# The last phase of a four-stage recurrent kernel: batches taken in pairs, gate products in seven block products, copies on ScalarE

## The chip, the cores and the metric

The kernel runs on one core of one Trainium2 chip. The metric is the device time of one execution in microseconds; the time before is the median of three runs, 1617.33 us (1615.9 to 1617.58).

## The reference, cut to what matters

Everything is float32, with batch 16, sequence 512 and width 512. Four residual stages follow one another.

```python
x = x + L0(x, cond)      # becomes x * (gate + 2): one multiplication in the kernel
x = x + L1(x, cond)      # h_t = tanh(x_t @ Wx + b + h_{t-1} @ Wh), 512 steps
x = x + L2(x, cond)      # gated linear recurrence, below
x = x + L3(x, cond)      # a layer of its own for every batch, below

# L2
f = sigmoid(x @ W_f.T + b_f); i = sigmoid(x @ W_i.T + b_i)
s = f + i + 1e-8
f, i = f / s, i / s
new = i * (x @ W_h.T + b_h)
log_cum = cumsum(log(f + 1e-8))
hidden = cumsum(exp(log_cum[-1] - padded(log_cum)[:-1]) * new) + exp(log_cum) * cond

# L3: rank-8 factors x_a, x_b of every batch from a small network over cond
layer = base + x_a @ x_b.T          # 512 x 512, per batch
out = x + x @ layer
```

Below, x2 is the sequence after L1 and x3 the one after L2.

## The kernel before

The kernel has two long parts. Widths lie on the 128 partitions in four chunks (`KC` = 4), time and batch on the free axis.

**The recurrence** (the loop over `n` in 64 blocks and `s` in 8 steps, up to about 909 us). At each step TensorE multiplies the state with `wh_sb` (L417), ScalarE takes the tanh (L609), VectorE transposes the result in four pieces (L610) and, at four of the eight steps, adds the states of two time steps into the tile x2 (L622), which stays in SBUF whole (16 batches of 4 x 512). TensorE's spare time in a step goes to the input products of a later block and to `early_gate`: the first steps of the gates of L2, for which x2 is already known. `SETS` says which, and `made_before(b, j)` returns the number of steps that batch b and chunk j have behind them (128 to 192). These normalized gates go to DRAM (`early`) through SP's queue. The order of instructions on TensorE, ScalarE, VectorE and SP is the order in which the code records them (`manual_schedule`); each of these engines works through its own list in order, and so does Pool.

**The last phase** takes one batch after the other, and in it four gate units (`gate_unit`, one for each chunk j of the output width). A unit makes three products (forget, input, candidate) of four matmuls each over the steps that are not made yet, into PSUM banks. ScalarE takes two sigmoids out of PSUM (L716) into `f` and `i`; SP fetches the early steps of both from DRAM (L715). VectorE then runs the chain L717 to L732: sum, reciprocal, normalization, candidate (read from PSUM, L722), three scans with a multiplication between them (L726, L729, L730, L732). Pool adds the two parts and x2 (L736, L737), which makes x3.

After the second unit of a batch, the output tiles of the batch before follow on TensorE: four tiles of four matmuls (L756), each copied out by ScalarE (L751) and stored by SP (L752) through two buffers `osb`. After the third unit the layer of this batch is made (`layer_of`: four rank-8 products, L535, and VectorE's addition of the base out of PSUM, L539). The first layer is made in the last step of the recurrence. The last batch's output is split so that only the last quarter of its products waits for the last chain.

Of the kernel before, what the change touches and what calls it, by code (L numbers as in the profile page):

```python
# [74 lines left out]
IDLE = (3, 12, 2)  # L75
EPS = 1e-8
# [7 lines left out]
def kernel(  # L84
# [47 lines left out]
    bias_a = dram.tile([R, D], F32, name="bias_a")  # L132
    factor = [dram.tile([BP, R, D], F32, name=f"factor_{i}") for i in range(2)]
# [311 lines left out]
    def early_gate(q, step):  # L445
# [18 lines left out]
        for c in range(KC):  # L464
            nc.tensor.matmul(  # L465
                ps[c * BP : (c + 1) * BP, :].rearrange("p (b t) -> p b t", **shape),
                w[:, k, j * P + c * BP : j * P + (c + 1) * BP],
                x2[:, k, batches, steps],
                start=(k == 0),
                stop=(k == KC - 1),  # L470
                skip_group_check=True,
            )
# [64 lines left out]
    def add_base(banks, layer):  # L537
        for c, pl in enumerate(banks):
            nc.vector.tensor_tensor(layer[:, c, :], pl, base_sb[:, c, :], ALU.add)  # L539

# [13 lines left out]
    BEGINS = {T - 1: 0, 0: 1, 2: 2}  # L556

# [7 lines left out]
    for n in range(NBLK):  # L565
# [3 lines left out]
        for s in range(T):  # L569
# [21 lines left out]
            if (n, s) == (NBLK - 1, T - 1):  # L591


                first_layer = [
                    new_bank(NBLK, i, "pl").rearrange("p g f -> p (g f)") for i in range(NBANK)
                ]
                first_layer.append(ps_q.tile([P, D], F32, tag="pg", name="pl_3"))
                make_layer(*first_rows, first_layer)
# [15 lines left out]
            if n == 0 and s == G - 1:  # L614
                opening.close()
                x2pool = ctx.enter_context(tc.tile_pool(name="x2pool", bufs=1, side="right"))
                x2 = x2pool.tile([P, KC, B, S], F32)
            if s == max(PAIRS[g]):
                t0, t1 = PAIRS[g]
                step = t1 - t0  # L620
                at = slice(n * T + t0, n * T + t1 + step // abs(step), step)
                nc.vector.tensor_tensor(  # L622
                    x2[:, :, :, at].rearrange("p k b t -> p k t b"),
                    xs[n][:, :, t0 // 2, :, :],
                    turned.rearrange("p k (t b) -> p k t b", t=2),
                    ALU.add,
                )
            elif n + 2 < NBLK:
                gated(nc.vector, xs[n + 2], xb, s)
# [25 lines left out]
            if (n, s) == (1, 0):  # L655

                end_layer(0)

# [10 lines left out]
        if n == NBLK - 4:  # L669
            at = w2pool.tile([P, P], F32, tag="b2", name="at_0", bufs=2)  # L670
            bt = w2pool.tile([P, D], F32, tag="w2", name="bt_0", bufs=AHEAD)
            first_rows = load_layer(0, at, bt)
        pre, nxt = nxt, ahead
    while urgent or pieces:
        do_pieces(S)

    add_base(first_layer, wx_sb)
    rnn.close()

    x3pool = ctx.enter_context(tc.tile_pool(name="x3pool", bufs=2))  # L680
    work = ctx.enter_context(tc.tile_pool(name="work", bufs=2))
    zero = work.tile([P, 1], F32, bufs=1)
    nc.gpsimd.memset(zero, 0.0)  # L683
    zeros = zero.to_broadcast([P, S])

    pools = {
        tag: ctx.enter_context(tc.tile_pool(name=f"ps_{tag}", bufs=1, space=PSUM))
        for tag in ("pl0", "pf", "pl1", "pi", "po0", "pc0", "po1", "pc1")
# [5 lines left out]
    def gate_unit(b, j, x3):  # L694
        ps = []
        te = made_before(b, j)
        for w_sb, tag in ((wf_sb, "pf"), (wi_sb, "pi"), (wc_sb, f"pc{j % 2}")):
            p = bank(tag, f"{b}_{j}")
            for k in range(KC):
                nc.tensor.matmul(  # L700
                    p[:, te:],
                    w_sb[:, k, j * P : (j + 1) * P],
                    x2[:, k, b, te:],
                    start=(k == 0),
                    stop=(k == KC - 1),
                )
            ps.append(p)
        pf, pi, pc = ps

        f = work.tile([P, S], F32, tag="f", name=f"f_{b}_{j}", bufs=3)  # L710
        i = work.tile([P, S], F32, tag="i", name=f"i_{b}_{j}")
        s = work.tile([P, S], F32, tag="s", name=f"s_{b}_{j}")
        old, new = slice(0, te), slice(te, S)
        for which, (gate, p, bias) in enumerate(((f, pf, C_BF), (i, pi, C_BI))):
            nc.sync.dma_start(out=gate[:, old], in_=early[b, which, j, :, old])  # L715
            nc.scalar.activation(gate[:, new], p[:, new], AF.Sigmoid, bias=col(bias, j))  # L716
        nc.vector.scalar_tensor_tensor(s[:, new], f[:, new], EPS, i[:, new], ALU.add, ALU.add)  # L717
        nc.vector.reciprocal(s[:, new], s[:, new])  # L718
        nc.vector.tensor_tensor(f[:, new], f[:, new], s[:, new], ALU.mult)
        nc.vector.tensor_scalar(f, f, EPS, None, ALU.add)  # L720
        nc.vector.tensor_tensor(i[:, new], i[:, new], s[:, new], ALU.mult)
        nc.vector.scalar_tensor_tensor(  # L722
            i[:, new], pc[:, new], col(C_BH, j), i[:, new], ALU.add, ALU.mult
        )

        nc.vector.tensor_tensor_scan(  # L726
            s[:, ::-1], f[:, ::-1], zeros, 1.0, ALU.mult, ALU.add
        )
        nc.vector.tensor_tensor(i, i, s, ALU.mult)  # L729
        nc.vector.tensor_tensor_scan(s, i, zeros, 0.0, ALU.add, ALU.add)  # L730

        nc.vector.tensor_tensor_scan(  # L732
            f, f, zeros, condT_sb[:, j, b : b + 1], ALU.mult, ALU.add
        )
        engine = nc.vector if (b, j) == (B - 1, KC - 1) else nc.gpsimd
        engine.tensor_tensor(s, s, f, ALU.add)  # L736
        engine.tensor_tensor(x3[:, j, :], s, x2[:, j, b, :], ALU.add)  # L737

    def layer_rows(b):
        at = work.tile([P, P], F32, tag="at", name=f"at_{b}", bufs=1)  # L740
        bt = work.tile([P, D], F32, tag="bt", name=f"bt_{b}", bufs=1)
        return load_layer(b, at, bt)

    def layer_of(b, at, bt, layer):
        banks = [bank(tag, f"{b}_layer") for tag in ("pl0", "pl1", "po0", "po1")]
        make_layer(at, bt, banks)
        add_base(banks, layer)

    def leave(b, t, po, tag="osb"):
        osb = work.tile([P, D], F32, tag=tag, name=f"osb_{b}_{t}")  # L750
# [3 lines left out]
    def output_part(po, t, x3, layer, ks):  # L754
        for k in ks:
            nc.tensor.matmul(  # L756
                po, x3[:, k, t * P : (t + 1) * P], layer[:, k, :], start=(k == 0), stop=(k == KC - 1)
            )

    def last_layer(b, x3, layer):  # L760
        for t in range(S // P):
            po = bank(f"po{t % 2}", f"{b}_{t}")
            output_part(po, t, x3, layer, range(KC))
            leave(b, t, po)

    layer = wx_sb
    pending = None
    for b in range(B):
        x3 = x3pool.tile([P, KC, S], F32, tag="x3", name=f"x3_{b}")
        end = b == B - 1  # L770
        if 0 < b < B - 1:
            factors = layer_rows(b)
        for j in range(KC):
            gate_unit(b, j, x3)
            if j == (KC - 1 if end else 1) and pending is not None:
                last_layer(*pending)
            if j == 2 and 0 < b < B - 1:
                layer_of(b, *factors, layer)
            if j == 0 and end:

                layer_of(B - 1, *layer_rows(B - 1), base_sb)
        pending = b, x3, layer


    last = S // P - 1
    pos = [bank(tag, "last") for tag in ("pl0", "pl1", "po0")]
    ends = [bank(tag, "end")[:, : D // 2] for tag in ("po1", "pi")]
    columns = [slice(n * D // 2, (n + 1) * D // 2) for n in range(2)]

    def last_rows(ks, n):  # L790
        for k in ks:
            nc.tensor.matmul(
                ends[n],
                x3[:, k, last * P :],
                base_sb[:, k, columns[n]],
                start=(k == 0),
                stop=(k == KC - 1),
            )

    for t, po in enumerate(pos):  # L800
        output_part(po, t, x3, base_sb, range(KC - 1))
    for n in range(2):
        last_rows(range(KC - 1), n)

    for t, po in enumerate(pos):
        output_part(po, t, x3, base_sb, (KC - 1,))
        leave(B - 1, t, po, ("osb", "i", "s")[t])
    for n, copy in enumerate((nc.vector.tensor_copy, nc.scalar.copy)):
        last_rows((KC - 1,), n)
        osb = work.tile([P, D // 2], F32, tag=("s", "osb")[n], name=f"osb_end_{n}")  # L810
        copy(osb, ends[n])
        (nc.sync, nc.scalar)[n].dma_start(out=out[B - 1, last * P :, columns[n]], in_=osb)


# [56 lines left out]
```

## Time and profile before

| | |
|---|---|
| median of three runs | 1617.33 us |
| span of the profiled execution | 1614.1 us (the 3.2 us beside it are start and end) |
| end of the recurrence (last addition into x2) | 909.25 us |
| last phase, from there to the end of the span | 704.8 us |
| busy share of TensorE, VectorE, ScalarE, Pool over the span | 99%, 70%, 26%, 11% |
| one batch of the last phase, start to start of the output tiles | 45.0 us (batches 1 to 7), 42.4 us (later) |
| granted clock of TensorE | 1.00 throughout |

A line of a group or a timeline names the start and the length in us, the engine, the line of the code, the operation, the tiles it writes and reads with their sizes, the number of records taken together, and in brackets how long the engine stood idle before and what it waited for. PE is TensorE, PEld its weight loads, DVE VectorE, ACT ScalarE, POOL GpSimd, SPq the queue of SP that issues transfers.

### The profile page before, as it was taken

The numbers are of one execution on the slowest core, as the hardware profiler recorded it, in microseconds if no ns is written. First come the engines' busy times: TensorE is split into PE (matmuls) and PEld (weight loads), VectorE is DVE, ScalarE is ACT, GpSimd is POOL, SyncE is SP. The second block draws the span as 40 slices with busy tenths as digits, with TensorE's granted clock in tenths as the row PEclk, the third lists the DMA queues.
The fourth block names the chain that finished last, engine by engine and source line by source line (L and its number), as shares of the span: only waits on it lengthen the run. The fifth ranks groups of instructions, "written<-read, shape, count | busy, mean of one in ns | idle before, by whom it ended". The sixth has DMA issues, their size and how long they took to land.

```text
span 1614.1 us, 67901 instructions
## 1 busy us (share of the span) xinstructions
PE 1603.6 (99%) x29328; PEld 1146.0 (71%) x29328; DVE 1132.3 (70%) x3618; ACT 424.9 (26%) x2484; POOL 172.6 (11%) x145
## 2 busy tenths in 40 slices
PE   9999999999999999999999999999999999999998
PEld 6888888888888888888888655555555555555564
DVE  4555655565556666666665798888888888988887
ACT  3333333333333333333333211111111111111111
POOL 0000000000000000000000022222222222222222
PEclk9999999999999999999999999999999999999999
DMA  7554431111111111111111101111111111111111
GB/s 228 148 147 128 121 105 46 36 31 36 37 37 37 37 37 37 37 37 31 37 39 30 29 21 43 33 43 39 43 40 44 44 46 39 31 44 47 37 44 58
DMA packets 128085, 88.11 MB, mean 55 GB/s; under 512 B 22645, under 2 KB 116633, under 8 KB 127785
## 3 DMA queue, kind: packets, MB, share of 16 engines
q1 hardware_dynamic: 79152, 55.05, 11.1%
q10 hardware_dynamic: 48632, 28.73, 6.2%
q8 instruction: 229, 3.75, 1.0%
q14 instruction: 72, 0.58, 0.1%
HBM read 55.67 MB, written 28.07 MB: 52 GB/s over the span
## 4 chain that ended last, share of the span: by engine, by line
PE 96%; DVE 2%; DMA 1%; issue 0%; SPq 0%; ACT 0%; ACTq 0%; DVEq 0%
PE pre L417 41%; PE po L756 13%; PE pg L465 13%; PE pf L700 9%; PE pc L700 9%; PE pi L700 9%; PE pf L380 1%; PE pl_layer L535 1%; DVE s L718 1%; DMA wh_sb<-in_wh_dram 1%; PE pl_last L756 0%; DMA xb<-in_xT_dram 0%; DVE s L726 0%; DVE s L730 0%; PE po_last L756 0%
## 5 line engine op out<-in xcount | busy, mean ns | idle before, releaser
L417 PEld LDWEIGHTS pre<-wh_sb,h_out 128*32 128x32 f32 x16384 | 466.7, 110 | 146.6 <-DVE h_out L610 143.4
L417 PE MATMUL pre<-wh_sb,h_out 128*32 128x128 f32 x16384 | 560.6, 273 | 2.4 <-DVE h_out L610 1.1
L610 DVE STREAM_TRANSPOSE h_out<-a 128x32 f32<-128x32 f32 x2048 | 264.6, 187 | 347.4 <-ACT a L609 345.9
L609 ACT ACTIVATE a<-pre 128x32 f32<-128x32 f32 x2048 | 238.0, 203 | 573.4 <-PE pre L417 572.7
L417 PE MATMUL pre<-wx_sb,x 128*32 128x128 f32 x8192 | 285.9, 273 | 1.0 <-DMA wx_sb<-in_wx_dram 0.5
L417 PEld LDWEIGHTS pre<-wx_sb,x 128*32 128x32 f32 x8192 | 239.0, 110 | 2.1 <-DMA wx_sb<-in_wx_dram 1.5
L756 PE MATMUL po<-wx_sb,x 128*128 128x512 f32 x480 | 209.0, 592 | 0.1
L756 PEld LDWEIGHTS po<-wx_sb,x 128*128 128x128 f32 x480 | 91.0, 190 | 111.6 <-issue 105.7
L700 PE MATMUL pf<-x,wf_sb 128*128 128x352 f32 (+3 forms) x512 | 165.3, 466 | 0.3 <-DVE x L622 0.3
L700 PE MATMUL pc<-x,wc_sb 128*128 128x352 f32 (+3 forms) x512 | 163.7, 463 | 1.3 <-DVE i L722 1.3
L700 PE MATMUL pi<-x,wi_sb 128*128 128x352 f32 (+3 forms) x512 | 163.6, 462 | 0.0
L718 DVE RECIPROCAL s<-s 128x368 f32<-128x368 f32 (+2 forms) x64 | 152.2, 2378 | 2.2
L700 PEld LDWEIGHTS pf<-x,wf_sb 128*128 128x128 f32 x512 | 96.0, 190 | 68.4 <-issue 15.8
L736 POOL TENSOR_TENSOR s<-s,f 128x512 f32<-128x512 f32 x63 | 86.5, 1374 | 509.9 <-DVE s L730 504.1
L700 PEld LDWEIGHTS pc<-x,wc_sb 128*128 128x128 f32 x512 | 97.2, 190 | 57.5 <-DVE i L722 1.9
L700 PEld LDWEIGHTS pi<-x,wi_sb 128*128 128x128 f32 x512 | 97.3, 190 | 55.9
L622 DVE TENSOR_TENSOR x<-x,h_out 128x128 f32<-128x128 f32 x256 | 101.2, 395 | 18.9 <-DMA wi_sb<-in_wiT_dram 0.2
L751 ACT COPY osb<-po 128x512 f32<-128x512 f32 x60 | 35.1, 585 | 263.4 <-PE po L756 144.9
L683 POOL MEMSET zero<- 128x1 f32 x1 | 0.1, 98 | 907.5 <-DVE wx_sb L539 907.5
L717 DVE SCALAR_TENSOR_TENSOR s<-f,i 128x368 f32<-128x368 f32 (+2 forms) x64 | 34.7, 543 | 88.1 <-ACT i L716 88.1
L716 ACT ACTIVATE f<-pf,vec_sb 128x368 f32<-128x368 f32 (+2 forms) x64 | 35.7, 558 | 215.2 <-PE pf L700 160.6
L465 PE MATMUL pg<-x,wc_sb 128*32 128x512 f32 (+1 forms) x640 | 84.2, 581 | 0.0
(113 smaller groups left out, 1270.8 us busy)
## 6 DMA issues: line engine op xcount, KB each, us to landing
out_dram<-osb SPq DMA_DIRECT2D x63, 256.0 KB
xb<-in_xT_dram ACTq DMA_DIRECT2D x61, 256.0 KB
w<-in_l3w_dram SPq DMA_DIRECT2D x72, 128.0 KB
w<-in_l3w_dram ACTq DMA_DIRECT2D x64, 128.0 KB
early<-ef SPq DMA_DIRECT2D x39, 128.0 KB
early<-ei SPq DMA_DIRECT2D x39, 128.0 KB
f<-early SPq DMA_DIRECT2D x16, 96.0 KB
i<-early SPq DMA_DIRECT2D x16, 96.0 KB
```

The source lines that it names most:

```text
L417: nc.tensor.matmul(pre[PLACE[g][0]][j * BP : (j + 1) * BP, PLACE[g][1], :], lhsT, tile_columns(w, j), start=False, stop=False, skip_group_ ...
L465: nc.tensor.matmul(ps[c * BP : (c + 1) * BP, :].rearrange("p (b t) -> p b t", **shape), w[:, k, j * P + c * BP : j * P + (c + 1) * BP], x2 ...
L609: nc.scalar.activation(a[:, at], pre[bank][:, place, at], AF.Tanh)
L610: nc.vector.transpose(turned[:, c, :], a[:, at])
L622: nc.vector.tensor_tensor(x2[:, :, :, at].rearrange("p k b t -> p k t b"), xs[n][:, :, t0 // 2, :, :], turned.rearrange("p k (t b) -> p k ...
L700: nc.tensor.matmul(p[:, te:], w_sb[:, k, j * P : (j + 1) * P], x2[:, k, b, te:], start=(k == 0), stop=(k == KC - 1),)
L716: nc.scalar.activation(gate[:, new], p[:, new], AF.Sigmoid, bias=col(bias, j))
L717: nc.vector.scalar_tensor_tensor(s[:, new], f[:, new], EPS, i[:, new], ALU.add, ALU.add)
L718: nc.vector.reciprocal(s[:, new], s[:, new])
L736: engine.tensor_tensor(s, s, f, ALU.add)
L751: nc.scalar.copy(osb, po)
L756: nc.tensor.matmul(po, x3[:, k, t * P : (t + 1) * P], layer[:, k, :], start=(k == 0), stop=(k == KC - 1))
```

## The change

Only the last phase is written anew; the recurrence gets another layout of x2 and stores.

- **Pairs and seven products.** Two batches are one left operand of two rows, the two halves of the width its two columns; the weights are a 2 x 2 block matrix. Six units a pair: F0 to F3 join the forget and input weights of a chunk, C0 and C2 the candidate weights of two chunks. A unit makes seven block products of two matmuls instead of eight. The four sums of input blocks are made once a pair (`sums_of`, on Pool, between the products of F3 of the pair before; on VectorE for pair 0), the combined weights once, in place (`make_weights`).
- **Running sums in PSUM, copied out.** Products 1, 6, 7, 4 add up in one bank (`al`), 5 and 3 in another (`be`), 2 stands alone (`ga`). After each product ScalarE copies the running sum to SBUF: into `got` (1, 6, 7) or `rest` (5, 2, 3). `add` then adds `rest` to `got`: on VectorE for F units, on Pool for C units. `rest_ring` has one buffer, the other rings have two. Two sets of banks (`al0`, `be0`, `ga0` and `al1`, `be1`, `ga1`) alternate between units.
- **The chain** works on two batches at once up to the scans, then six scans; the second scan multiplies inside, and the multiplication that stood between the scans goes to Pool with the two additions, three Pool instructions for two batches.
- **Layers** are copied from PSUM by ScalarE and the base is added by Pool; the fourth bank of a layer is `po1`. Output tiles are spread over the units as fillers, one quarter at each 0 of `USUAL`. The first layer moves from the recurrence into the last phase.
- **x2 in DRAM.** x2 is now laid out batch first. Batches 6 to 15 are also stored to `kept` during and after the recurrence (`keep_part`, on SP's queue); their place in SBUF becomes working memory, and five pairs are fetched back into a ring of four slots. x3 of a pair overwrites x2 of the pair before.

The diff, cut to its core:

```diff
+    def keep_part(batches, steps):
+        nc.sync.dma_start(out=kept[...], in_=x2[:, batches, :, steps])
+    keeping = {}
+    for first, part in enumerate((slice(0, 128), slice(128, 256), slice(256, 384))):
+        for b in range(KEPT, B):
+            keeping[20 + 14 * first + b - KEPT, 6] = slice(b, b + 1), part
+    for b in range(KEPT, B):
+        keeping[60 + (b - KEPT) // 4, 2 * ((b - KEPT) % 4)] = slice(b, b + 1), slice(384, 480)
...
-                x2 = x2pool.tile([P, KC, B, S], F32)
+                x2 = x2pool.tile([P, B, KC, S], F32)
...
+            if (n, s) in keeping:
+                keep_part(*keeping[n, s])
...
+    for b in (*range(KEPT + 2, B, 2), KEPT):
+        keep_part(slice(b, b + 2), slice(480, S))
...
+    f_ring = Ring(carve(2, S), carve(2, S))
+    four_ring = Ring(four_a, carve(4, NB))
+    three_ring = Ring(three_a, carve(3, NB))
+    rest_ring = Ring(rest_a)
+    osb_ring = Ring(carve(D), carve(D))
...
+        def product(self, which):
+            ...
+            ps = {1: self.al, 6: self.al, 7: self.al, 4: self.al, 5: self.be, 3: self.be, 2: self.ga}[which]
+            for k in range(2):
+                nc.tensor.matmul(ps, w[:, k, :], src[:, k, :], start=(k == 0 and which in (1, 5, 2)), ...)
+            if which == 4:
+                if self.gates:
+                    nc.scalar.activation(self.f[:, 1, new], ps, AF.Sigmoid, bias=col(C_BF, self.j))
+                else:
+                    nc.scalar.copy(self.got[:, 2, n], ps)
+                return
+            to = {1: self.spots[0], 6: self.spots[1], 7: self.spots[2],
+                  2: self.rest[:, 0], 3: self.rest[:, 1], 5: self.rest[:, 2]}[which]
+            nc.scalar.copy(to[:, n], ps)
+        def add(self):
+            if self.gates:
+                nc.vector.tensor_tensor(self.got[:, :, n], self.got[:, :, n], self.rest[:, :, n], ALU.add)
+            else:
+                nc.gpsimd.tensor_tensor(two, two, self.rest[:, 0:2, n], ALU.add)
+                nc.gpsimd.tensor_tensor(one, one, self.rest[:, 2, n], ALU.add)
+        def squash(self):
+            nc.scalar.activation(self.f[:, 0, new], self.got[:, 0, n], AF.Sigmoid, bias=col(C_BF, j))
+            nc.scalar.activation(self.i[:, :, new], self.got[:, 1:3, n], AF.Sigmoid, bias=col(C_BI, j))
...
+    def chain(unit, cand_unit, final=False):
+        v = nc.vector
+        v.scalar_tensor_tensor(s[:, :, new], f[:, :, new], EPS, i[:, :, new], ALU.add, ALU.add)
+        v.reciprocal(s[:, :, new], s[:, :, new])
+        v.tensor_tensor(f[:, :, new], f[:, :, new], s[:, :, new], ALU.mult)
+        v.tensor_scalar(f, f, EPS, None, ALU.add)
+        v.tensor_tensor(i[:, :, new], i[:, :, new], s[:, :, new], ALU.mult)
+        v.scalar_tensor_tensor(i[:, :, new], cand, col(C_BH, j), i[:, :, new], ALU.add, ALU.mult)
+        for b in range(2):
+            v.tensor_tensor_scan(s[:, b, ::-1], f[:, b, ::-1], zeros, 1.0, ALU.mult, ALU.add)
+            v.tensor_tensor_scan(i[:, b], i[:, b], f[:, b], 0.0, ALU.add, ALU.mult)
+            v.tensor_tensor_scan(f[:, b], f[:, b], zeros, condT_sb[...], ALU.mult, ALU.add)
+            if not final and b == 0:
+                continue
+            ...
+            e.tensor_tensor(i[:, at, : S - 1], i[:, at, : S - 1], s[:, at, 1:], ALU.mult)
+            e.tensor_tensor(i[:, at], i[:, at], f[:, at], ALU.add)
+            e.tensor_tensor(x3[:, at, j, :], i[:, at], x[:, at, j, :], ALU.add)
...
+    USUAL = (1, 5, 0, 6, 2, 0, 7, 3, 0, 4, 0)
...
+            c0 = new("C0")
+            queue_tile(6, p - 2)
+            run(c0, USUAL, {2: [before["F3"].squash]})
+            fill(4)
+            chain(before["F3"], before["C2"])
+            c0.add()
+            f0 = new("F0")
+            queue_tile(7, p - 2)
+            run(f0, USUAL)
+            fill(4)
+            f0.add()
+        f1 = new("F1")
+        queue_tile(0, p - 1)
+        run(f1, USUAL, {2: [f0.squash]} if p else {})
+        fill(4)
+        chain(f0, c0)
+        f1.add()
+        if p:
+            layer_of(2 * p - 1, sides[0])
+            queue_tile(1, p - 1)
+            fill(4)
+        c2 = new("C2")
+        queue_tile(2, p - 1)
+        run(c2, USUAL, {2: [f1.squash]})
+        fill(4)
+        chain(f1, c0)
+        c2.add()
+        f2 = new("F2")
+        queue_tile(3, p - 1)
+        run(f2, USUAL)
+        fill(4)
+        f2.add()
+        f3 = new("F3")
+        queue_tile(4, p - 1)
+        hooks = {2: [f2.squash]}
+        ...                                  # sums of the next pair, on Pool
+        run(f3, USUAL, hooks)
+        fill(4)
+        chain(f2, c2)
+        f3.add()
+        layer_of(2 * p, sides[0])
+        queue_tile(5, p - 1)
+        fill(4)
```

`run` records a unit's products in the order of `USUAL`; a 0 stands for one quarter of an output tile, and a hook is recorded right after the copy of the product whose number it has.

## The prediction

> **What bounds the kernel now.** I read the page's busy times first, then the chain that ended last, then the timeline of the last phase (from 909.4 us on) engine by engine. Busy time, then the chain's two lines:
>
> ```profile
> PE 1603.6 (99%) x29328; PEld 1146.0 (71%) x29328; DVE 1132.3 (70%) x3618; ACT 424.9 (26%) x2484; POOL 172.6 (11%) x145
> ...
> PE 96%; DVE 2%; DMA 1%; issue 0%; SPq 0%; ACT 0%; ACTq 0%; DVEq 0%
> ```
>
> TensorE never rests, in the recurrence or after it. The last phase in one stretch (length, then busy PE, PEld, DVE, ACT, POOL, then clock, DMA share, GB/s):
>
> ```profile
> 930.00:1290.00 360.00, 360.00 (x1098) 197.99 (x1097) 306.77 (x354) 54.50 (x97) 88.64 (x66) 1.00 0.12 39
> ```
>
> PE 100%, VectorE 85%, Pool 25%, ScalarE 15%: an edit that takes products away helps only while VectorE, and what is handed between engines, keeps pace. TensorE's timeline for part of a batch:
>
> ```profile
> 1127.22 2.74 PE L700 MATMUL pf<-x,wf_sb 128*128 128x384 f32 x8
> 1129.80 2.74 PE L700 MATMUL pi<-x,wi_sb 128*128 128x384 f32 x8
> ...
> 1134.96 13.90 PE L756 MATMUL po<-wx_sb,x 128*128 128x512 f32 x32
> 1148.69 2.64 PE L700 MATMUL pf<-x,wf_sb 128*128 128x368 f32 x8
> ```
>
> A matmul of the code is two records. From start to start, four of 384 columns take 2.58 us (0.645 each, 1.68 ns a column) and sixteen of 512 take 13.73 (0.858 each). VectorE's timeline of one gate unit (one batch, one chunk, 384 columns):
>
> ```profile
> 915.45 0.56 DVE L717 SCALAR_TENSOR_TENSOR s<-f,i 128x384 f32<-128x384 f32 x1 [2.88 <-ACT i L716]
> 916.04 2.55 DVE L718 RECIPROCAL s<-s 128x384 f32<-128x384 f32 x1
> ...
> 921.69 0.69 DVE L729 TENSOR_TENSOR i<-i,s 128x512 f32<-128x512 f32 x1
> 922.29 1.28 DVE L732 TENSOR_TENSOR_SCAN f<-f,condT_sb,zero 128x512 f32<-128x512 f32 x1
> ...
> 924.61 0.53 DVE L717 SCALAR_TENSOR_TENSOR s<-f,i 128x384 f32<-128x384 f32 x1
> ```
>
> One unit is 9.16 us, L717 to L717.
>
> **Products: -56 us of TensorE.** Before, columns of gate products sum to 273,408 (12 a unit, widths 512 minus `made_before`). After: six units a pair, seven products of two matmuls, 240,128. At 1.68 ns: 458 against 402 us. Output tiles (256 matmuls, 219.7 us) and layers (about 1.07 us each) stay. TensorE's own sum is 402 + 220 + 17 = 639 us, against the 704.7 that the phase takes now.
>
> **VectorE: less in all, but in bigger lumps.** A chain now serves two batches. Two units of 9.16 are 18.3; two L729 leave for Pool (0.6 each, start to start), and six instructions start once instead of twice (about 0.1 each): 16.4 us at 384 columns, 15.0 at 320. Each F unit adds one addition of 1152 columns, 1.3 us (1.04 ns a column, from 0.55 us at 384). Layer additions (0.65 us each) go to Pool. Some 69 us a pair: alone no bound.
>
> **The wait that the change adds.** `rest_ring` holds one buffer. Every unit's copy of product 5 writes it, so it waits until the unit before has been added. For C units that addition stands on Pool, in order behind the three Pool instructions of a chain, and these wait for that chain's last scans on VectorE. The built program shows it: the copy of product 5 of F0 and of F2 waits for Pool, and on ScalarE the copies of products 6 and 7 are queued behind it; TensorE's product 7 accumulates onto the bank that copy 6 must first empty, and everything of TensorE's is behind product 7. So two times a pair the engines run one after another. At 384 columns, from one squash to the next but one:
>
> - squash on ScalarE, 0.58 and 0.90 us, overlapping: 1.3
> - chain on VectorE: 16.4
> - Pool: three of 1024 columns and C's addition of 1152. The two rows (minimum/median/maximum):
>
> ```profile
> L736 POOL TENSOR_TENSOR s<-s,f x60: 1260/1425/1501, 933.9 to 1574.8; 128x512 f32<-128x512 f32 x60
> L737 POOL TENSOR_TENSOR x<-s,x x63: 1260/1266/1432, 926.3 to 1595.1; 128x512 f32<-128x512 f32 x63
> ```
>
>   At 1.26 us for 512: 3 x 2.52 + 2.8 = 10.4. At L736's median it would be 11.7.
> - two copies on ScalarE: 0.9
> - TensorE: products 7, 3, 4, then 1, 5, 6, 2 of the next unit (7 x 1.29) and three quarters of a tile (3 x 0.86), then a copy of 0.5: 12.1
> - hand-overs, six of about 0.08: 0.5. Sum 41.6.
> - then the next squash 1.3, chain 16.4, F1's addition 1.3 (on VectorE, behind the chain) and the copies of products 5, 6 and 2 behind it, 1.3: 20.3. TensorE has one unit, a layer and a tile beside this, 18: hidden.
>
> 61.9 us for half a pair, which is one batch; a batch takes 45.0 now (output groups start 45.0 apart early, 42.4 later). The second half with 368 and 352 columns gives 59 to 60, so a pair 121; the later pairs (320 columns first) 115.
>
> The Trainium skill ("GPSIMD Engine Reference", Specifications) says that Pool shares its SBUF interfaces with VectorE and suffers from instructions with two inputs there. L736's 1.43 beside L737's 1.27 agrees. In the stretch that counts VectorE stands idle, so I take the lower row; the upper adds 16 x 1.3 = 21 us.
>
> **Start, first pairs, end.** Pair 0 has no tiles and only one such hand-over (C2 to F2), but VectorE first builds the combined weights (24 subtractions of 256 columns at 0.34; the 16 last ones delay the first chain by 5.5). First chain at 18, two chains with addition and squash 35, Pool and copies 12, then the rest of F2, F3 and the layer 13: about 80. Pair 1: 121 plus 5, since its first tile needs pair 0's last chain. After pair 7: two tiles, a layer and 32 output matmuls (36 us) around the last chain, then 4 for copy and store (now 1610.5 to the end): 49 with some waiting. Sum: 80 + 126 + 2 x 121 + 4 x 115 + 49 = 957 us, against 704.7.
>
> **A cold TensorE.** The gaps before product 7 are about 16 us, 15 of them. No row of before shows such a pause later on, but the start does: the same bf16 product over and over, first and last:
>
> ```profile
> 1.31 1.46 PE L263 MATMUL idle<-blank 128*128 128x512 bf16 x3 [1.31 <-POOL blank L243]
> 6.86 0.81 PE L263 MATMUL idle<-blank 128*128 128x512 bf16 x3
> ```
>
> One record of them lasts 0.61 us at first and 0.38 at last, so they start (1.46 - 0.61)/2 = 0.425 us apart, then (0.81 - 0.38)/2 = 0.215, though the granted clock reads 1.00 in both. The slow rate lasts until about 6.6, that is 3.4 us of the stretch that begins at 3.24, or 5.3 from the first. A restart costs 0 to 2.6 us; I take 1.7 (half of 3.4): 15 x 1.7 = 26, bounds 0 and 39.
> The Trainium skill ("TensorE: Matmul & The Clock Gate", Part 1) says that an idle window of about 3.4 us returns the array to half rate, and so speaks against this change; by it the restarts cost an estimated 26 us too, by the clock column nothing.
>
> **The recurrence: +38 us.** Thirty stores to `kept` are issued at step 6 of blocks 20 to 29, 34 to 43 and 48 to 57. In the built program each waits for that step's addition into x2 (L622 before), and the next step's addition, on VectorE, waits for the store, though they touch different steps. Behind it stand the transposes that TensorE's next step needs. VectorE in the recurrence, and a 256 KB store with the copy that waited for it:
>
> ```profile
> 430.81 0.39 DVE L622 TENSOR_TENSOR x<-x,h_out 128x128 f32<-128x128 f32 x1
> 431.91 0.49 DVE L610 STREAM_TRANSPOSE h_out<-a 128x32 f32<-128x32 f32 x4 [0.71 <-ACT a L609]
> 432.44 0.39 DVE L622 TENSOR_TENSOR x<-x,h_out 128x128 f32<-128x128 f32 x1
> ```
>
> ```profile
> 1015.60 3.27 SPq L752 DMA_DIRECT2D out_dram<-osb  x3
> ```
>
> ```profile
> 1017.93 0.59 ACT L751 COPY osb<-po 128x512 f32<-128x512 f32 x1 [6.84 <-DMA out_dram<-osb]
> ```
>
> Store to release is 2.33 us. So the second addition starts 0.39 + 0.1 + 2.33 + 0.1 = 2.9 us after the first, not 1.63: 1.27 late, 30 x 1.27 = 38. Lower bound 0 (all absorbed); upper 60, if 512-byte pieces land in 3 us.
>
> **At nothing.** The ten stores of 96 steps carry no such wait; the last five delay early loads and copies within pair 0's 18 us (if not: up to 8). Five fetches of 2 MB go behind a pair's last store on SP's queue; early loads and stores behind them have some 40 us. ScalarE's copies total some 200 us of 950.
>
> **Sum.** By the profiled execution: 909.4 + 38 + 957 + 26 = 1930 us of span. The median of the runs, 1617.33, is 3.2 above that span: **1933**.
>
> **Rivals.** (1) C's addition is early enough and the stores cost nothing: TensorE's 639, plus 14 waits of 1.8 where tile 1 or 5 needs the bank that a layer's fourth copy empties, 15 at the start and 10 at the end, 689 against 704.7: 1602, faster. It needs Pool to be done within the 9 us from C's product 2 to the next unit's product 5; the sum above puts it at 28. Against it stand 16.4 of VectorE alone. 3%. (2) The same with the stores' waits: 1640. 4%. (3) The serial chain, but TensorE stays slow over its whole share in it: 12 more at each of 15 in place of the 26: about 2090. 4%. (4) The serial chain without the stores' waits or without cold restarts: 1869 to 1907, inside the forecast's range.
>
> **How the numbers follow.** The forecast, 1933 with 89%. Low end 1845: no store waits (-38), no cold restarts (-26), 24 for chains and Pool that are 2.5% shorter. High end 2000: stores 60 (+22), cold 39 (+13), Pool at the upper row (+21), 11 for the start. A measurement here tells about 0.2% (3 us) from no change; rival 1 alone is faster, and hardly anything lies between: faster 0.03, same 0.01, slower 0.96.
>
> **What would show it.** Right: ScalarE's copy of a product 5 waits for Pool about 19 us, 15 times; TensorE waits 15 to 17 before product 7 of F0 and F2; pairs of 115 to 126; Pool starts a chain's first instruction right after VectorE's last scans; L629 waits for stores 30 times. Wrong: a phase with TensorE over 90% busy, or a bound on VectorE with hardly a wait for Pool.

## The result, and the profile after

The changed kernel takes 2030.05 us (median of four runs, 2026.75 to 2036.91) against 1617.18 for the kernel before beside it: 1.256 times as long (95% interval 1.253 to 1.259). Slower as forecast, but 97 us beyond the 1933 of the prediction and 30 above the high end of its range. The profiled span is 2028.7 us. The last addition into x2 ends at 960.1 us (909.25 before), and the last phase takes 1068.6 us (704.8 before). So 51 us of the 415 lie in the recurrence and 364 in the last phase.

The page's busy times and its chain of the work that ended last, in the changed kernel:

```profile
PE 1634.4 (81%) x29128; PEld 1137.9 (56%) x29128; DVE 1190.9 (59%) x3357; ACT 579.0 (29%) x2820; POOL 411.4 (20%) x208
...
DVE 5%; PE 4%; POOL 1%; ACT 1%; issue 1%; DMA 0%; POOLq 0%; ACTq 0%; DVEq 0%
```

TensorE is no longer the chain: what ends last passes from engine to engine. (The shares do not add up to the span, since the chain was followed back over a part of the last phase only.) A stretch of the last phase (length, then busy PE, PEld, DVE, ACT, POOL, granted clock, DMA share, GB/s):

```profile
1100.00:1900.00 800.00, 548.18 (x1524) 295.98 (x1525) 479.63 (x313) 200.25 (x408) 310.22 (x145) 0.83 0.12 40
```

PE 69%, VectorE 60%, Pool 39%: no engine is full, which is what a serial path looks like. The table of waits names it (engine, line, what it waited for: us in total, times, longest):

```profile
POOL x L900 <- DVE x L892: 492.8, 32, 33.3
...
PE al_F L827 <- ACT three_a L846: 268.2, 15, 20.3
...
ACT rest_a L846 <- POOL x L855: 173.2, 8, 22.6
ACT rest_a L846 <- POOL four_a L855: 151.1, 7, 22.1
...
DVE x L629 <- DMA kept<-x: 53.7, 30, 3.0
```

Read from below: ScalarE's copy of product 5 of F0 and F2 waits 15 times, 21.6 us each, for C's addition on Pool; TensorE stands 17.9 us before product 7 behind that; Pool's L900 waits for VectorE's scans. That is the ring of waits that the prediction drew. What it did not draw is in the timelines of VectorE and of Pool for one half pair, F3 of pair 2 and F0 of pair 3:

```profile
1338.83 2.77 DVE L882 SCALAR_TENSOR_TENSOR x<-x 128x704 f32<-128x704 f32 x1 [2.62 <-ACT x L861]
...
1351.98 1.28 DVE L893 TENSOR_TENSOR_SCAN x<-x,condT_sb,zero 128x512 f32<-128x512 f32 x1
...
1355.53 3.12 DVE L893 TENSOR_TENSOR_SCAN x<-x,condT_sb,zero 128x512 f32<-128x512 f32 x1
...
1383.20 0.96 DVE L882 SCALAR_TENSOR_TENSOR x<-x 128x768 f32<-128x768 f32 x1 [9.08 <-ACT x L861]
```

```profile
1338.50 2.35 POOL L902 TENSOR_TENSOR x<-x 128x1024 f32<-128x1024 f32 x1
...
1355.58 2.00 POOL L900 TENSOR_TENSOR x<-x 128x1022 f32<-128x1022 f32 x1 [9.46 <-DVE x L892]
1358.88 2.34 POOL L901 TENSOR_TENSOR x<-x 128x1024 f32<-128x1024 f32 x1 [1.31 <-DVE x L893]
```

The same scan of 512 columns takes 1.28 us for the first batch and 3.12 for the second. The second has Pool's L900 beside it, from 0.05 us after its start, and ends 1.07 us after L900 does: it stood still for 1.84 us, nearly all of Pool's 2.00. L882 takes 2.77 beside Pool's L902, and 0.96 for more columns with Pool idle. The sum of such lengthenings over VectorE's lines L882, L884 to L886 and L893 (their busy time less their count times the undisturbed length at each width) is 96 us in this kernel.

TensorE at the end of that half pair's pause:

```profile
1367.29 2.93 PE L827 MATMUL al_F<-sum,weights 128*128 128x384 f32 x4 [17.29 <-ACT three_a L846]
1370.01 2.16 PE L827 MATMUL be_F<-sum,wi_sb 128*128 128x384 f32 x4
1372.00 1.02 PE L928 MATMUL po<-x 128*128 128x512 f32 x2
```

From start to start 2.72 and 1.99 us for four records that take 1.29 elsewhere: 2.1 us lost after this pause. Over the 15 pauses it is 1.5 to 2.7 us, 33 in all.

### The profile page after: what moved, and what is told of

Its sections match the earlier page's. It is cut to its first block, busy times and chain, and to the rows that moved or that the text cites. A ratio compares the mean times of both kernels' runs of the same rounds, so it can differ in the third digit from the quotient of the medians.

```text
span 2028.7 us, 67676 instructions
## 1 busy us (share of the span) xinstructions
PE 1634.4 (81%) x29128; PEld 1137.9 (56%) x29128; DVE 1190.9 (59%) x3357; ACT 579.0 (29%) x2820; POOL 411.4 (20%) x208
## 5 line engine op out<-in xcount | busy, mean ns | idle before, releaser
L827 PE MATMUL al_F<-sum,x 128*128 128x368 f32 (+3 forms) x192 | 76.9, 528 | 142.6 <-ACT three_a L846 142.6
L900 POOL TENSOR_TENSOR x<-x 128x1022 f32<-128x1022 f32 (+1 forms) x32 | 63.0, 1968 | 492.8 <-DVE x L892 492.8
L882 DVE SCALAR_TENSOR_TENSOR x<-x 128x768 f32<-128x768 f32 (+3 forms) x32 | 59.0, 1844 | 166.2 <-ACT x L861 166.2
L883 DVE RECIPROCAL x<-x 128x768 f32<-128x768 f32 (+3 forms) x32 | 147.3, 4603 | 1.1
L851 DVE TENSOR_TENSOR three_a<-three_a,rest_a 128x1104 f32<-128x1104 f32 (+2 forms) x16 | 20.5, 1284 | 210.9 <-ACT rest_a L846 206.8
L629 DVE TENSOR_TENSOR x<-x,h_out 128x128 f32<-128x128 f32 x256 | 100.7, 393 | 71.9 <-DMA kept<-x 53.7
L893 DVE TENSOR_TENSOR_SCAN x<-x,condT_sb,zero 128x512 f32<-128x512 f32 x64 | 140.8, 2200 | 2.3
L928 PE MATMUL po<-wx_sb,x 128*128 128x512 f32 x224 | 126.1, 665 | 14.9 <-ACT x L913 14.9
L928 PE MATMUL po<-x 128*128 128x512 f32 x224 | 121.6, 650 | 14.9 <-ACT wx_sb L913 14.9
L827 PE MATMUL be_F<-sum,wi_sb 128*128 128x384 f32 (+3 forms) x256 | 100.6, 521 | 2.1 <-DVE sum L872 2.1
L901 POOL TENSOR_TENSOR x<-x 128x1024 f32<-128x1024 f32 (+1 forms) x32 | 87.3, 2727 | 41.7 <-DVE x L893 39.3
L473 PE MATMUL pg<-x,wf_sb 128*32 128x512 f32 (+1 forms) x640 | 84.9, 593 | 13.4 <-DVE x L629 13.4
```

What stands on the lines that cost most here:

```text
L473: nc.tensor.matmul(ps[c * BP : (c + 1) * BP, :].rearrange("p (b t) -> p b t", **shape), w[:, k, j * P + c * BP : j * P + (c + 1) * BP], x2 ...
L629: nc.vector.tensor_tensor(x2[:, :, :, at].rearrange("p b k t -> p k t b"), xs[n][:, :, t0 // 2, :, :], turned.rearrange("p k (t b) -> p k ...
L827: nc.tensor.matmul(ps, w[:, k, :], src[:, k, :], start=(k == 0 and which in (1, 5, 2)), stop=(k == 1), skip_group_check=True,)
L882: v.scalar_tensor_tensor(s[:, :, new], f[:, :, new], EPS, i[:, :, new], ALU.add, ALU.add)
L883: v.reciprocal(s[:, :, new], s[:, :, new])
L893: v.tensor_tensor_scan(f[:, b], f[:, b], zeros, condT_sb[:, j, 2 * p + b : 2 * p + b + 1], ALU.mult, ALU.add)
```

## The experiments

Each run is one timing beside one of the kernel before (1618.3, 1618.7, 1619.1 and 1624.2 us in the four sets), so differences under 5 us are not read. The recurrence is the same in the changed kernel, e1, e2, e4 and e5, and it ended between 954.9 and 968.6 us in them, so between these the phase is compared, not the whole. "Phase" is the span after the last addition into x2. "Lengthening" is the sum just described; the first row of the table is the kernel as changed.

| run | time, us | recurrence ends | phase | lengthening |
|---|---|---|---|---|
| changed kernel | 2030.1 | 960.1 | 1068.6 | 96 |
| e1_c_first | 1808.6 | 968.6 | 838.2 | 162 |
| e2_rest2 | 1837.4 | 956.2 | 879.5 | 100 |
| e3_keep7 | 1982.9 | 910.1 | 1071.0 | 97 |
| e4_mul_v | 2008.6 | 959.6 | 1047.3 | 38 |
| e5_warm | 2000.3 | 954.9 | 1043.6 | 96 |
| e6_free | 1727.1 | 909.1 | 816.2 | 163 |
| e7_free_mul | 1708.5 | 910.6 | 796.1 | 91 |
| e8_free_all | 1767.8 | 911.6 | 854.3 | 70 |
| e9_layer_pe | 1739.0 | 911.4 | 825.9 | 19 |
| e10_layer_sums | 1755.3 | 910.2 | 843.3 | 11 |
| e11_layer_pe2 | 1700.3 | 913.2 | 785.3 | 27 |
| e12_po_first | 1664.3 | 914.1 | 748.4 | 30 |

(For e8 it includes L887 and L851, which collide only there.)

**The order on Pool (e1_c_first).**

```diff
-            chain(before["F3"], before["C2"])
             c0.add()
+            chain(before["F3"], before["C2"])
...
-        chain(f1, c0)
         c2.add()
+        chain(f1, c0)
```

> C0's and C2's additions are recorded ahead of the chain that stood before them, so on Pool they no longer stand behind three instructions that wait for VectorE's last scans; nothing else changes. Theory (the order on Pool makes the serial path): ScalarE's copy of product 5 of F0 and F2, which waited 21.6 us for Pool 15 times, waits under 5; the 6.7 us of Pool's three, the 2.8 of C's addition and most of the 12 us of TensorE's products leave the path of each half pair, some 16 to 20 of its 67: 15 x 16 to 20 = 240 to 300 less, 1730 to 1790 in all, and the granted clock goes back to about 1.00 as the gaps of TensorE go. Rival (the waits at the copies only mark time that VectorE's chains and what collides with them need anyway): under 100 less, over 1930, with VectorE busy over 85% of the last phase.

The phase fell by 230 us, the whole by 221 to 1808.6, between the two expectations but close to the theory. TensorE's pauses before product 7 of the F units fell from 268 us to 17; those on the bank `al` of the C units rose from 36 to 73, behind copies that now wait longer for VectorE's additions out of the single buffer. The granted clock rose to 0.92, not to 1.00. The rival's condition came true as well: VectorE is busy 87% of the phase, and its lengthening rose from 96 to 162 us, since C's addition and the layers' now fall beside other work of VectorE. The order made the serial path; what it hid is VectorE and Pool.

**The single buffer (e2_rest2).**

```diff
-    both, turned_s = carve(NB), carve(2, NB)
+    rest_b = carve(3, NB)
...
-    rest_ring = Ring(rest_a)
+    rest_ring = Ring(rest_a, rest_b)
```

> A second buffer in rest_ring, the order on Pool unchanged. Theory (the single buffer puts TensorE's products on the path, the order on Pool puts the rest there): products 5, 6 and 7 of F0 and F2 no longer wait for C's addition, but those of the unit behind them do; of each half pair only TensorE's 12 us leave the path, and the pause before product 7 moves to F1 and F3: 15 x 12 = 180 less, about 1850. Rival (the buffer alone makes the serial path): the waits of product 5 for Pool go for good, 1730 to 1790 as with the additions ahead. Second rival (the buffer does not matter): within 30 of 2030.

1837.4: the theory. The waits for Pool stay, 15 of them, shorter and one unit later (the second edge is now the buffer of F1 and F3):

```profile
ACT rest_a L846 <- POOL four_a L855: 80.2, 7, 14.0
ACT x L846 <- POOL x L855: 79.4, 8, 12.5
```

Either edit alone takes out most of the same wait; the gains, 230 and 189 us of phase, do not add.

**The stores (e3_keep7).**

```diff
-            keeping[20 + 14 * first + b - KEPT, 6] = slice(b, b + 1), part
+            keeping[20 + 14 * first + b - KEPT, 7] = slice(b, b + 1), part
```

> The thirty stores of 128 steps are issued one step of the recurrence later, after step 7 of the block in place of step 6, so that the next addition into x2 comes several steps after the store. Theory (the addition of the very next step waits for the store): the waits of L629 for a store, 30 in the changed kernel, go, and the recurrence ends 51 us earlier, near 909; the last phase stays 1069; 1979 in all. Rival (the stores' traffic itself, or the other layout of x2, costs the 51 us): L629's waits go or move, but the recurrence still ends near 960, and the whole stays near 2030.

The theory in full: L629 waits for no store, the recurrence ends at 910.1, the phase is as it was. The stores' traffic and the other layout of x2 cost nothing that shows. In the changed kernel one of the thirty looks like this, the second addition 3.62 us after the first, where 1.63 is usual:

```profile
400.90 0.40 DVE L629 TENSOR_TENSOR x<-x,h_out 128x128 f32<-128x128 f32 x1
...
404.52 0.37 DVE L629 TENSOR_TENSOR x<-x,h_out 128x128 f32<-128x128 f32 x1 [2.03 <-DMA kept<-x]
```

**One Pool instruction to VectorE (e4_mul_v).**

```diff
-            e.tensor_tensor(i[:, at, : S - 1], i[:, at, : S - 1], s[:, at, 1:], ALU.mult)
+            v.tensor_tensor(i[:, at, : S - 1], i[:, at, : S - 1], s[:, at, 1:], ALU.mult)
```

> Only the first of Pool's three instructions of a chain, the product of 1024 columns (L900), goes to VectorE, where it comes after the last scan; so no Pool instruction runs beside the scan of L893 for the second batch. Theory (a VectorE instruction with two inputs stands still while a Pool instruction runs): that scan takes 1.28 us for both batches in place of 1.28 and 3.12; VectorE gains 32 x 1.84 = 59 and pays about 32 x 1.1 = 35 for the product, and Pool's 2.0 leave the path of 16 half pairs, 32: about 56 less, 1974. L882 beside Pool's later instructions stays at 2.8. Rival (the second batch's scan is slow for a reason of its own, its place or its operands): it stays at 3.12, and the whole stays within 10 of 2030.

The mechanism is as the theory has it: the lengthening fell from 96 to 38 us, nearly all of it in L893, and L882 beside Pool's later instructions stays at 2.8. The row of L893 in this kernel (minimum, median and maximum of its 64 lengths in ns; 1283/2160/3121 in the changed kernel):

```profile
L893 DVE TENSOR_TENSOR_SCAN x<-x,condT_sb,zero x64: 1283/1284/2106, 997.3 to 1987.5; 128x512 f32<-128x512 f32 x64
```

The gain was 21 us and not 56: my expectation took the scan's delay and Pool's 2.0 us off the path one after the other, but they are the same time. From the last L893's start to Pool's L901 it was 3.35 us in the half pair shown; here it is 2.53 (1.20 for the scan, 1.33 from L900's start on VectorE to L901's): 0.8 less, 32 times, 26 us.

**The cold TensorE (e5_warm).**

```diff
+    def spin(unit):
+        tag = "ga1" if unit.side == 0 else "ga0"
+        ps = bank(tag, f"{unit.name_}_spin")
+        for _ in range(18):
+            nc.tensor.matmul(ps, wx_sb[:, 0, :P], wx_sb[:, 1, :], start=True, stop=True)
...
+            elif step == 7 and unit.name in ("F0", "F2") and unit.p:
+                spin(unit)
+                unit.product(step)
```

> Ahead of product 7 of F0 and F2, 18 matmuls of 512 columns into a free bank, their result unused: at 0.858 us each they fill 15.4 of the 17.9 us for which TensorE stood still there. Theory (TensorE restarts slowly after the pause): product 7, whose four records took 2.72 us from start to start in the changed kernel, and product 3, 1.99, take 1.29 each, as everywhere else; 2.1 us less at each of 15, 32 less, about 1998, and the granted clock of the last phase rises from 0.83 towards 1.00. Rival (what is slow there is not the pause, but the read of the bank that ScalarE has just emptied, or of what Pool has just written): 2.72 and 1.99 stay, and the whole stays within 8 of 2030.

```profile
1354.80 1.56 PE L827 MATMUL al_F<-sum,weights 128*128 128x384 f32 x4 [1.85 <-ACT three_a L846]
1356.19 1.45 PE L827 MATMUL be_F<-sum,wi_sb 128*128 128x384 f32 x4
1357.48 1.02 PE L928 MATMUL po<-x 128*128 128x512 f32 x2
```

Start to start 1.39 and 1.29: behind this pause, cut to 1.85 us, the slow restart is gone, and the clock of the stretch 1100 to 1900 reads 0.96. The phase is 25 us shorter (the recurrence, which this edit does not touch, happened to be 5 shorter). Not every restart went: pair 0's pause is not filled, and five filled ones that were left at 2.85 to 3.45 us still lost 1.4 to 1.8 us each. Products 7 and 3 together lost 33 us before and 11 here, so 22 of the 25 us are theirs; the pause itself is the cause.

**Both waits and the stores gone (e6_free).** The edits of e1, e2 and e3 together.

> The additions of C0 and C2 ahead, a second rest buffer and the stores one step later, together. Theory (VectorE's instructions with two inputs and Pool's run one after another, and only the reciprocal, 4.95 us, lies beside Pool): a chain without collisions is 16.4 and its addition 1.3, of which 12.8 cannot lie beside Pool; Pool has 12.9 for a quarter of a pair (four chains of 6.7, two additions of 2.8, four sums of 2.15, two layers of 5.3, over four). 25.7 x 32 = 822 at the worst, and less by what VectorE stands idle anyway: a last phase of 790 to 830 after 909, 1705 to 1745 in all, hardly under the kernel with only the additions ahead less its store waits. Rival (with both waits gone TensorE or VectorE's own 17.7 bounds): a phase of 680 to 720, 1595 to 1635, about the kernel before.

1727.1, in the middle of the theory's range and over 90 us above the rival's. With the serial path gone the kernel is still 108 us slower than before. VectorE is now nearly full (728 of 808 us), 163 us of it lengthening; Pool has 450 us of work:

```profile
912.00:1720.00 808.00, 705.77 (x1977) 374.87 (x1975) 727.89 (x446) 264.30 (x526) 446.04 (x190) 0.91 0.15 48
```

**Which of Pool's work to move (e7_free_mul, e8_free_all).** From e6: e7 has e4's edit too; e8 has all three instructions of each chain on VectorE:

```diff
-            e = v if final and b == 1 else nc.gpsimd
+            e = v
```

> The same as the run with both waits and the store waits gone, and the product of each chain (L900) on VectorE. Theory of VectorE and Pool taking turns: 1.2 more for VectorE and 2.0 less for Pool, 0.8 x 32 = 26 less than that run. Rival (VectorE's own length bounds): 1.2 x 32 = 38 more than it.

> The same, and all three of Pool's instructions of each chain on VectorE (about 1.2, 1.1 and 1.1 there for 2.0, 2.34 and 2.34 on Pool). Theory of VectorE and Pool taking turns: 12.8 + 3.4 for VectorE and 12.9 - 6.7 for Pool make 22.4 that cannot overlap, and VectorE's own length 21.1: 32 x 21.1 to 22.4 and 55 for start and end, a phase of 730 to 775, 1645 to 1690 in all, 40 to 80 less than with them on Pool, though VectorE, the busier engine, gets 108 us more work. Rival: those 108 us come on top of the run with them on Pool.

e7: 18.6 less, the sign and roughly the size of the theory. e8: 41 *more* than e6, where I had expected 40 to 80 less; neither expectation holds. My sum added all of Pool's time and forgot which part lies beside the reciprocal. In e7 one chain shows it, VectorE and then Pool:

```profile
1313.20 1.48 DVE L882 SCALAR_TENSOR_TENSOR x<-x 128x640 f32<-128x640 f32 x1 [1.42 <-ACT x L861]
1314.71 4.15 DVE L883 RECIPROCAL x<-x 128x640 f32<-128x640 f32 x1
```

```profile
1310.79 3.21 POOL L901 TENSOR_TENSOR x<-x 128x1024 f32<-128x1024 f32 x1 [10.05 <-DVE x L900]
1314.08 2.80 POOL L902 TENSOR_TENSOR x<-x 128x1024 f32<-128x1024 f32 x1
```

L901 lies beside VectorE's wait for the squash and L902 beside the reciprocal, which reads one operand and takes 4.15 us with or without Pool beside it. They cost VectorE little: 16 of e7's 91 us of lengthening lie beside these two lines. Moving them there adds 84.5 us to VectorE (L901 and L902, 85.9 in its rows of e8 less 1.4 of the last chain) and takes 21 of lengthening away; 64, and the phase rose by 58.

**The layers' additions off Pool (e9, e10, e11, e12).** From e7. e9 adds `base_sb` on TensorE, as a product with the identity in the layer's bank, ahead of each eight-row product; e11 issues the four identity products first (its edit is the one shown):

```diff
-        make_layer(at_sb, bt_sb, banks)
+        for c, pl in enumerate(banks):
+            nc.tensor.matmul(pl, ident, base_sb[:, c, :], start=True, stop=False, skip_group_check=True)
+        for c, pl in enumerate(banks):
+            rows = slice(c * BP, c * BP + R)
+            nc.tensor.matmul(pl, at_sb[rows, :], bt_sb[rows, :], start=False, stop=True, skip_group_check=True)
         for c, pl in enumerate(banks):
             nc.scalar.copy(layer[:, c, :], pl)
-        for h in range(2):
-            at = slice(2 * h, 2 * h + 2)
-            nc.gpsimd.tensor_tensor(layer[:, at], layer[:, at], base_sb[:, at], ALU.add)
```

e10 is e9 with the sums of later pairs on VectorE, e12 is e11 with ScalarE's copy of `po1` first:

```diff
-                    lambda p=p, which=which: sums_of(p + 1, which, nc.gpsimd)
+                    lambda p=p, which=which: sums_of(p + 1, which, nc.vector)
```

```diff
-        for c, pl in enumerate(banks):
+        for c, pl in sorted(enumerate(banks), reverse=True):
             nc.scalar.copy(layer[:, c, :], pl)
```

> From the run with the waits gone and the product on VectorE: Pool's 32 additions of the layers go, TensorE adds base_sb into the layers' banks as a product with the identity (64 matmuls of 512 columns, 0.858 each, 55 us more). Theory of VectorE and Pool taking turns: in that run VectorE's L882, L884, L885 and L886 are 91 us longer than undisturbed, some 70 of it (L884 to L886) beside the layers' additions and the sums; about half of that goes, and Pool's chain of work gets shorter: 30 to 65 less, 1645 to 1680. Rival (TensorE, 640 and now 55 more, has become the bound): no gain or up to 55 more than 1708.

> The same, and the four sums of each later pair on VectorE too (28 instructions of about 0.95 us each, 27 us, for 28 of 1.8 to 2.5 on Pool). Theory of VectorE and Pool taking turns: 27 more for VectorE, up to 60 less of Pool beside it, of which what lay beside a reciprocal or an idle VectorE is no gain: between 20 less and 10 more than without this step; the collisions of L884 to L886 fall under 10 us. Rival (collisions are not what makes those lines long): they stay as long.

> As the run that adds base_sb on TensorE, but the four products with the identity are issued first and the layer's four products of eight rows after them, so that these stand side by side again. Theory (in that run the eight-row products, 0.7 us for all four side by side and 1.05 each between the others, made TensorE the bound: 8 x 1.05 = 8.4 for a layer, where 4 x 0.86 + 1.1 = 4.5 were meant): 3.9 x 16 = 62 less, 1677, with TensorE still busy over 92% of the last phase. Rival (the identity products themselves, or a wait behind them, cost the time): within 10 of 1739.

> The same, and ScalarE empties the layer's fourth bank, po1, first, since the next matmul of an output tile waits for it. Theory (TensorE is the bound, so a wait of its own counts in full): the wait of L928 for ScalarE's last copy of a layer, 2.1 us where the four eight-row products stand together, 14 times, falls to about 0.6; 14 x 1.5 = 21 less than the run before it. Rival (VectorE and Pool bound again, TensorE's wait is slack): no change, within 5.

e9: the lengthening fell from 91 to 19, more than expected, and the time rose by 31: the rival, TensorE 96% busy in the phase. Its layer, in e9 and then in e11:

```profile
1330.70 1.12 PE L914 MATMUL al_layer<-bt_sb,at_sb 8*128 8x512 f32 x2
1331.75 1.12 PE L913 MATMUL be_layer<-base_sb,ident 128*128 128x512 f32 x2
1332.81 1.12 PE L914 MATMUL be_layer<-bt_sb,at_sb 8*128 8x512 f32 x2
```

```profile
1366.01 0.69 PE L915 MATMUL po_layer<-bt_sb,at_sb 8*128 8x512 f32 x1
...
1369.25 5.40 PE L929 MATMUL po<-x 128*128 128x512 f32 x8 [2.12 <-ACT wx_sb L917]
1374.48 1.24 PE L827 MATMUL al_C<-x,wc_sb 128*128 128x320 f32 x4
```

Between others, an eight-row product takes 1.05 us and so does the identity product beside it; in a row the four eight-row ones start within 0.03 us of each other and are over in 1.1. e10: 16 us more than e9, 6 beyond what either view allowed. L884 to L886 are back at their undisturbed lengths, as expected, but 14 of the 28 sums take 2.65 us each on VectorE in place of 0.95, which is Pool again beside them, and TensorE is the bound anyway. Its own busy time grew by 16 us, at a granted clock of 0.93 in place of 0.96; why is not shown. e11: 39 less than e9, not 62, because ScalarE's copies, hidden behind e9's long layer, are waited for again (29.8 us, 4.7 + 4.7 in e9): 62 - 20 = 42. e12: 36 less, not 21: the wait fell from 2.12 to 0.78, and the tile behind it, whose eight records took 5.23 us in the tile of e11 shown (1369.25 to 1374.48) and 4.9 to 6.6 in twelve of the fourteen, takes 3.54 in all. 14 x 1.34 = 19 and 21 for the tiles make 40, most of it found.

No version beats the kernel before: e12 is the nearest, 1664.3 beside its 1624.2, with TensorE 95% busy in its last phase. TensorE's own sum there is 639 plus 16 x 3.4 for the identity products, so the products' saving of 56 is spent again.

## Why the prediction was right or wrong

- **Direction and the serial wait: right.** The wait it named is there 15 times, 21.6 us (about 19 forecast); TensorE's pause is 17.9 (15 to 17). e1 and e2 show both halves of it, the order on Pool and the single buffer.
- **The step that failed: the chain on VectorE and Pool's share in it.** The prediction set Pool beside L736's rows, cited the Trainium skill ("GPSIMD Engine Reference", Specifications) on the SBUF interfaces that Pool shares with VectorE, and then wrote "In the stretch that counts VectorE stands idle, so I take the lower row". It asked only whether Pool gets slower. The first of Pool's three runs beside the last scan, and the last of them, or a layer's addition, beside the next chain's L882; there VectorE stands still: of the 96 us, 58 lie beside L900, 23 beside L902 and 14 beside the layers' additions. The term is in no bound of its range. That page speaks of contention between the two engines, which these rows bear out, and the row that I set beside it, Pool's own length, was the wrong one: it shows what Pool loses, not what VectorE does.
- Its half pair by terms, forecast (first chain scaled to 352 columns) and measured in the half pair shown, in us, from squash to squash but one:

  | term | forecast | measured |
  |---|---|---|
  | squash | 1.3 | 1.4 |
  | first chain, to the end of its last scan | 15.7 | **19.8** |
  | Pool after it (L900 lay inside the scan that it stopped) | 10.4 | **7.7** |
  | copies | 0.9 | 1.0 |
  | TensorE with the cold restart, and hand-overs | 14.3 | 14.4 |
  | squash | 1.3 | 1.5 |
  | second chain | 16.4 | **18.6** |
  | F1's addition and copies | 2.6 | 2.4 |
  | sum | 62.9 | 66.8 |

  In the first chain the stopped scan is no net loss, since L900 had to run there anyway (chain and Pool together 27.5 for 26.1); L882's 1.9 us there and the scan's 1.8 in the second chain are. Another 0.4 in each chain is no collision: it was sized that much too short.
- **The sum of it.** From F0's squash of pair 1 (1113.72) to F2's of pair 7 (1963.70) thirteen half pairs took 65.4 us each; the forecast has 59.1 and 1.7 for the restart: 4.6 x 13 = 60 too little, evenly over the pairs (134 measured for 121 + 3.4, later 127 to 132 for 115 + 3.4). The first chain began 25.8 us into the phase, not 18: 8 more, all before its squash (behind the squash the subtractions held it up by 5.3, 5.5 forecast), among them VectorE's wait of 2.6 for a store to `early`. The phase is 86 beyond its 983; the other 18, in the rest of pair 0 and at the end, stay open.
- **Recurrence: mechanism right, size small.** 51 measured, 38 forecast: a store held the next addition up by 1.70 us more than usual, not 1.27. Settled by e3.
- **Cold TensorE: right, a little small.** 2.2 each on average, 1.7 forecast. The profile does show it in the granted clock (0.83 over the stretch), which it did not at the start of the kernel before; the Trainium skill ("TensorE: Matmul & The Clock Gate", Part 1) gives an idle window of about 3.4 us and half rate. Product 7's 2.72 us for 1.29 agrees with the half rate. A limit at 3.4 us is not what e5 shows: of its six pauses from 2.85 to 2.94 us four were followed by the slow rate.
- **Rival 1 stands on a false condition.** It said that an early addition and free stores give 1602. e6 has both and takes 1727: TensorE would have been 689, but VectorE was busy for 729 of the phase's 816 us, 163 of them lengthening beside Pool. So "alone no bound" for VectorE's 69 us a pair was wrong too, once Pool's work is set beside it.
- **Small slips in its sums** (16.5 for 16.4 in the chain, 459 and 403 for 458 and 402 in the products) move nothing.

## What to carry to other kernels

Work moved from VectorE to Pool is off VectorE only where VectorE meanwhile waits or runs something that does not collide, or where its instruction has started first; set Pool's instructions against VectorE's in time, one by one, before counting the move as a gain. When a buffer's reader sits on an engine that works in order, look at everything recorded ahead of it there: here two lines in another order were worth 221 us. And a saving on the bounding engine is worth nothing until the engine that takes the work over has been summed with its collisions.

## What the hardware showed

- VectorE instructions with two operands, and a plain TENSOR_SCALAR of 1024 columns (L885, 0.69 us, up to 2.72 beside Pool), stand still until a Pool instruction ends that started before them, or within 0.05 us after them (L893). RECIPROCAL does not (4.95 us at 768 columns, in company or alone).
- Where VectorE's instruction has started clearly earlier, it is Pool that waits. Here L882 starts 0.17 us before one of Pool's sums and keeps its length; the sum takes 2.42 us in place of 1.81:

```profile
1181.77 0.93 DVE L882 SCALAR_TENSOR_TENSOR x<-x 128x736 f32<-128x736 f32 x1 [8.60 <-ACT x L861]
```

```profile
1181.94 2.42 POOL L872 TENSOR_TENSOR sum<-x 128x768 f32<-128x768 f32 x1 [1.35 <-PE al_F L827]
```

In the same way L901, 2.34 us alone, takes 3.0 to 3.3 behind an L851 that started 0.3 us earlier and keeps its 1.1 to 1.3. In the traces of the changed kernel and its variants no overlap of more than 0.15 us goes against these two points.
- TensorE's slow restart followed all 15 pauses of 16 to 20 us before product 7. For short pauses the runs show no sharp limit: those of 1.9 us and less before product 7 lost 0.1 us in e5; two of 2.57 and 2.58 us in e5 were not followed by the slow rate, four of 2.62 us in e4 were; of the six from 2.85 to 2.94 us in e5 four were.
- Eight-row products seem to keep the clock up less than full ones, though no run tests this by itself. After 1.1 us of them and 2.12 of waiting, twelve of e11's fourteen tiles took 4.9 to 6.6 us in place of 3.54; after 1.1 us and 0.78 of waiting none did (e12). In e9, where they stand in turn with full ones, eight of fourteen tiles were slow (4.9 to 5.9 us) after a wait of only 0.68.
